# Second layer's probabilities turned by DMA and bounded by ScalarE, fourth layer's mask added by VectorE, maxima turned in one transpose

## The chip, the cores and the metric

The kernel runs on one core of one Trainium2 chip. The time is device microseconds of one execution of the whole program; lower is better. A core has five engines that run their own instruction queues in order: TensorE (matmuls and transposes into PSUM; its weight loads are listed apart as PEld), VectorE (DVE), ScalarE (ACT), GpSimd (POOL) and SyncE (SP), whose queue here issues all DMAs. An engine stops at an instruction whose inputs are not there, and everything behind it in that queue waits too.

## The reference, cut to what matters

Four layers of attention and feed-forward follow one another on `x` of 16 batches x 128 tokens x 256 features, with 16 heads of 16 features. Only the second and the fourth layer, and the softmax of the third, matter here.

The second layer quantizes: scores of rounded queries and keys, a softmax, and the probabilities rounded to whole numbers from 0 to 255 before the product with the rounded values.

```
def _fq(x, delta, zp, n_bits):
    xi = _round_ste(x / delta) + zp
    xq = jnp.clip(xi, 0.0, 2.0 ** n_bits - 1.0)
    return (xq - zp) * delta
...
sim = einsum(_fq(q, dq, 128., 8), _fq(k, dk, 128., 8)) * SCALE
attn = softmax(sim)
out = einsum(_fq(attn, dw, 0.0, 8), _fq(v, dv, 128.0, 8))
```

This attention comes twice in the layer, first of the tokens to themselves, then to the context. The third layer adds a mask times -1e9 to the scores (a 128 x 128 mask in its first attention, one row of keys for each batch in its second). The fourth layer's second attention puts minus infinity where a 128 x 128 boolean mask is set:

```
scores = einsum('bhqd,bhkd->bhqk', q, k) * scale
if mask is not None:
    scores = jnp.where(mask[None, None], -jnp.inf, scores)
attn = softmax(scores)
out = einsum('bhqk,bhkd->bhqd', attn, v)
```

## The kernel before, in words

The 16 batches are worked in 8 groups of two (`GB = 2`), so a tile of tokens is 128 partitions x 2 x 256. `group(g)` lists a group's whole way through the four layers as steps. A step names an engine (or several that could do it), an assumed duration, the blocks it reads and writes, and a function that issues its instructions. All eight groups may be under way at once (`LIVE = 8`).

The order on every engine is fixed when the program is built. `Plan.order` plays the steps through with their assumed durations, always takes the ready step that could begin first (then by its level plus a number from the table `LEADS`, one for each group and stage), and gives it a place in memory. SBUF data lie in one `arena` of 348 units of 512 bytes a partition; each section of a group's work says how many buffers of a kind (`e`, `eT`, `eb`, `mt`, `w`) it may hold. A step on SP ends, for the plan, 2.2 us (`LOAD`) after its assumed duration, plus what the step names as its fourth entry. PSUM has four `pw` slots of 2 KB a partition and one `ps` slot of 8 KB, which holds all 16 heads' scores of one batch.

The second layer (`quantized_attention`, then `attention`) takes each of the two batches of a group in two halves of 8 heads, `c = 0, 1`: 2 attentions x 8 groups x 2 batches x 2 halves are 64 halves and 32 batches. For a half:
- TensorE has made the scores in `ps` (L833, bf16); VectorE takes the maxima (L1099) and subtracts them into `e` (L1112); ScalarE makes exponentials (L1118); VectorE makes the sums and their inverses (L1124 to L1127); POOL multiplies by them and adds `MAGIC` = 12582912.0, which rounds to a whole number (L1133).
- VectorE bounds the result at 255, takes `MAGIC` off again and writes bf16 into `eb` (L1137).
- TensorE turns the 8 heads' squares into a `pw` slot (L905), ScalarE or VectorE copies them out to `eT` (L910, L911).
- When both halves are there, TensorE multiplies with the values in `products` (L879): 16 bf16 matmuls of 128 columns, four at a time side by side on 32 columns of the array each. ScalarE scales the result by `dwv` (L1143).

The third and fourth layers use `plain_attention` (4 attentions, 64 batches in all). For a batch it makes the scores twice: queries on the partitions, to find each query's maximum for each head, then keys on the partitions with the maxima already taken off, so that the exponentials need no turn. In between the 16 maxima of each query are split into three bf16 pieces (`split`, L1261 to L1264), which lie in `mq` as four squares of 128 columns; four transposes (L1271) and one copy (L1275) bring them to `mt`. Four bf16 matmuls of 512 columns with the constant `three` (L844, from `laid`) then lay the negated maxima into all of `ps`, and the f32 scores accumulate onto them (L833). `laid` and the scores work on four strips of 32 partitions at a time.

Masks come in two ways. With `mask` (third layer's first attention) VectorE adds it while it moves the scores from `ps` to `e` or `eT` (L1246, L1295); the maxima are then taken from `e` (L1251) and the exponentials from `eT` (L1299). With `masked` and `masked_T` TensorE lays the mask into `ps` ahead of the scores, as a product with `ident_b` (L844); the maxima (L1236) and the exponentials (L1302) then read `ps`. The fourth layer's second attention does the latter, with the mask `m3` and its turned form `m3T` in bf16; there a row may have all keys masked, and one small instruction (L1239) puts such maxima to zero.

Of the kernel before, what the change touches and what calls it, by code (L numbers as in the profile page):

```python
# [16 lines left out]
P = 128  # L17
# [49 lines left out]
SLOTS = {"sm": (64, 46), "row": (128, 12), "pw": (2048, 4), "ps": (8192, 1), "mq": (1024, 4)}  # L67
# [8 lines left out]
    [83, 27, 167, 130, 306, 193, 74, 226, 213, -45, 163, -53, 159, -84, 116, -64, 214, 400, 286, 283],  # L76
    [-69, -856, -114, -260, -60, 57, -165, -14, -2, -22, -386, -90, 144, -71, -260, -59, -586, -159, -213, -106],
    [49, -47, -11, 314, -162, 407, 51, 168, -361, -27, -172, 141, -4, -107, 36, 5, -54, 235, 78, 92],
    [-16, -228, 250, -173, -19, 106, 36, 203, -176, 14, 164, 2, 299, -144, 10, 309, -45, 154, 150, -1],
    [210, 166, 422, 222, 201, 790, 324, 499, 569, 334, 435, 116, 502, 205, 259, 760, 536, 716, 652, 178],  # L80
    [330, 158, 210, 147, 392, 517, 262, 488, 490, 57, 292, 77, 380, 208, 348, 38, 542, 447, 523, 1141],
    [267, 148, 130, 158, 333, 376, 220, 605, 204, -29, 43, 216, 340, 164, 196, 435, 324, 999, 754, 951],
    [288, 156, 593, 320, 407, 313, 255, 389, 233, 323, -30, 86, 440, 164, 213, 583, 372, 760, 452, 550],
# [344 lines left out]
def decoder_stack_kernel(ctx: ExitStack, tc: tile.TileContext, a: dict, out: bass.AP):  # L428
# [19 lines left out]
    G.memset(magic, MAGIC)  # L448

# [40 lines left out]
    m3 = const.tile([P, S], BF16, tag="m3", name="m3")  # L490
    m1T = const.tile([P, S], F32, tag="m1T", name="m1T")
    m3T = const.tile([P, S], BF16, tag="m3T", name="m3T")
# [3 lines left out]
    three = const.tile([P, P], BF16, tag="three", name="three")  # L496
    mod = const.tile([P, 32], F32, tag="mod", name="mod")
# [28 lines left out]
    def prepare():  # L526
# [5 lines left out]
        def steps_of_quantization():  # L532
# [8 lines left out]
            V.tensor_tensor(dwv, d[:, :, 2], d[:, :, 3], ALU.mult)  # L541

# [6 lines left out]
        def masks():  # L549
# [4 lines left out]
            G.tensor_tensor(three, three, mod[:, 2:3].to_broadcast([P, P]), ALU.add)  # L554

            G.tensor_scalar(m1, m1, -1.0e9, 1.0, ALU.mult, ALU.mult)

        step([("POOL", 2.5, masks)], reads=[raw, dl_token], writes=[mask_token], least=110.0)


        for dst, n, src, eye, dtype in ((m1T, S, m1, ident, F32), (kmT, B, km, ident[:B, :B], F32), (m3T, S, m3, ident_b, BF16)):
# [305 lines left out]
    def products(eTs, vz, j, po, ones=False):  # L867

        def issue():
            for c in range(2):
                for i in range(2):
                    for s in range(4):
                        if ones:
                            lhsT = ones2[:, i, :]
                        else:
                            lhsT = vz.ap()[:, j, 4 * c + s, 2 * i : 2 * i + 2, :].rearrange("p a d -> p (a d)")
                        T.matmul(  # L879
                            po.ap()[32 * s : 32 * s + 32, 2 * ones + c, :], lhsT=lhsT,  # L880
                            rhs=eTs[c].ap()[:, 2 * s + i, :], start=(i == 0), stop=(i == 1),
                        )

        return issue

    def attention(x, wo, begin, soft, out_of, vz, dtype, after):


        plan.enter(after=after, w=1, oT=1, e=2, eT=2, **({"r": 1} if dtype == F32 else {"eb": 1}))
        wo = weight(wo)  # L890
        oT = block("m", [P, 2, NT], role="oT")
        for j in range(GB):
            ps, held = begin(j)
            eTs = []
            for c in range(2):
# [3 lines left out]
                per = 4 if dtype == F32 else 8  # L899
                for q0 in range(0, 8, per):  # L900
                    pt = block("pw", [P, per, S], dtype)

                    def turn(pt=pt, e=e, q0=q0):
                        for q in range(per):
                            T.transpose(pt.ap()[:, q, :], e.ap()[:, q0 + q, :], ident if dtype == F32 else ident_b)  # L905
# [291 lines left out]
    def plain_attention(x, qxT, kvT, ws, biases, mask=None, masked=None, cost=0.9, masked_T=None, key_mask=None, held=(), may_be_empty=False, there=None):  # L1197
# [29 lines left out]
        def batch(j):  # L1227
# [52 lines left out]
            def below(ps, mt=mt):  # L1280
                if masked_T is not None:
                    laid(ps, *masked_T)
# [187 lines left out]
```

## Time and profile before

| | |
|---|---|
| Time, median of 3 runs | 1461.03 us (1458.67 to 1462.03) |
| The profiled execution's own time | 1458.82 us |
| Its span, first to last instruction | 1456.7 us |
| TensorE busy | 1398.3 us, 96% of the span |
| VectorE busy | 1010.9 us, 69% |
| ScalarE busy | 849.7 us, 58% |
| POOL busy | 633.3 us, 43% |
| Mean granted TensorE clock | 0.993 |
| DMA, mean | 75 GB/s |

A profile is one execution taken by the hardware profiler. A line of it names the engine, the line of the program, the operation, the tile that is written and those that are read with their shapes (partitions x elements, or rows x columns of the array for TensorE), and a count; then the busy time, the mean duration in ns of one, and the idle time of the engine just before, with what ended it. Matmuls are pipelined, so a block's duration contains its drain, and the start of the next block comes earlier than its end. An f32 matmul or weight load shows as two instructions.

### The profile page before, as it was taken

How to read it: one execution, taken by the hardware profiler on the slowest of the kernel's cores; microseconds unless marked ns; L12 is line 12 of the kernel's file. 1: busy time of each engine (PE TensorE's matmuls, PEld its weight loads, DVE VectorE, ACT ScalarE, POOL GpSimd, SP SyncE). 2: the span in 40 equal slices, each digit the busy share in tenths (PEclk: the TensorE clock that was granted, in tenths of full speed). 3: DMA queues.
4: the chain of work that ended last, by engine and by line, in shares of the span. 5: the costliest groups of instructions: out<-in, count | busy, mean ns of one | idle time of the engine just before them, and what ended most of it. 6: DMA issues, size and time to landing. Idle time of an engine off the chain costs nothing. (4 is left out here: it accounts for less than half of the span.)

```text
span 1456.7 us, 35756 instructions
## 1 busy us (share of the span) xinstructions
PE 1398.3 (96%) x14771; PEld 1141.3 (78%) x14771; DVE 1010.9 (69%) x1555; ACT 849.7 (58%) x1490; POOL 633.3 (43%) x1415
## 2 busy tenths in 40 slices
PE   8899998999899999899999999999999999999998
PEld 6677887878678888687878777777878888787777
DVE  1665788898988779767764976779478766556431
ACT  4565676766776656565554665657556454445552
POOL 2232857455777446524432542545634234243210
PEclk9999998999999999999999999999999999999999
DMA  6566513412432122112211532211210111100000
GB/s 207 138 171 192 188 48 102 117 34 67 125 90 95 44 67 70 56 52 66 84 38 45 160 101 97 85 55 56 73 45 2 42 38 66 31 31 2 2 9 23
DMA packets 138386, 109.67 MB, mean 75 GB/s; under 512 B 72288, under 2 KB 127472, under 8 KB 138096
## 3 DMA queue, kind: packets, MB, share of 16 engines
q1 hardware_dynamic: 138224, 107.40, 24.5%
q8 instruction: 116, 1.90, 0.5%
q14 instruction: 46, 0.38, 0.1%
HBM read 80.11 MB, written 27.26 MB: 74 GB/s over the span
## 5 line engine op out<-in xcount | busy, mean ns | idle before, releaser
L688 PE MATMUL pw<-arena 128*128 128x256 f32 x2048 | 484.2, 387 | 7.3 <-ACT arena L654 3.1
L675 PE MATMUL pw<-arena 128*128 128x256 f32 x2048 | 480.9, 385 | 7.8 <-ACT arena L663 2.5
L688 PEld LDWEIGHTS pw<-arena 128*128 128x128 f32 x2048 | 383.0, 192 | 68.8 <-issue 9.3
L675 PEld LDWEIGHTS pw<-arena 128*128 128x128 f32 x2048 | 379.2, 191 | 71.0 <-issue 10.0
L1133 POOL TENSOR_SCALAR arena<-arena,sm 128x128 f32<-128x128 f32 x512 | 195.9, 403 | 107.7 <-DVE sm L1127 73.4
L1314 DVE RECIPROCAL arena<-pw 128x256 f32<-128x256 f32 x64 | 112.1, 1752 | 104.0 <-PE pw L879 86.8
L734 POOL TENSOR_TENSOR arena<-arena,rows 128x512 f32<-128x512 f32 x107 | 137.7, 1289 | 89.7 <-ACT arena L721 74.0
L833 PE MATMUL ps<-arena 32*128 32x128 f32 (+2 forms) x3328 | 153.0, 309 | 2.8 <-DVE arena L1112 1.1
L1236 DVE TENSOR_REDUCE sm<-ps 128x16 f32<-128x2048 f32 x48 | 109.6, 2283 | 36.3 <-PE ps L833 33.8
L833 PEld LDWEIGHTS ps<-arena 32*128 32x128 f32 x3072 | 116.1, 186 | 20.4 <-issue 12.0
L696 DVE TENSOR_TENSOR arena<-pw,arena 128x512 f32<-128x512 f32 x88 | 60.3, 685 | 101.2 <-PE pw L688 99.7
L801 ACT ACTIVATE arena<-pw,cols_sb 128x256 f32<-128x256 f32 x184 | 78.0, 472 | 68.3 <-PE pw L675 65.5
L1261 POOL CAST mq<-sm 128x16 bf16<-128x16 f32 x58 | 15.8, 273 | 234.2 <-DVE sm L1236 114.6
L710 POOL TENSOR_SCALAR sm<-sm 128x2 f32<-128x2 f32 x88 | 20.6, 234 | 215.0 <-DVE sm L705 200.1
L721 ACT ACTIVATE arena<-arena,sm,sm 128x256 f32<-128x256 f32 x149 | 83.2, 597 | 49.3 <-POOL sm L714 48.7
L663 ACT ACTIVATE arena<-pw,cols_sb 128x256 f32<-128x256 f32 x140 | 72.7, 563 | 50.5 <-PE pw L647 47.0
L1275 ACT COPY arena<-pw 128x512 bf16<-128x512 bf16 x64 | 37.3, 582 | 84.5 <-PE pw L1271 77.6
L879 PE MATMUL pw<-arena 128*32 128x128 f32 (+1 forms) x2560 | 82.9, 265 | 3.4 <-ACT arena L910 3.0
L1099 DVE TENSOR_REDUCE sm<-ps 128x8 f32<-128x1024 f32 x64 | 77.6, 1213 | 9.8 <-PE ps L833 9.5
L1302 ACT ACTIVATE arena<-ps 128x1024 f32<-128x1024 f32 x64 | 64.1, 1025 | 33.1 <-PE ps L833 30.3
L647 PE MATMUL pw<-ident,arena 128*128 128x128 f32 x416 | 66.8, 286 | 15.1 <-DMA arena<-in_x_dram 5.1
L910 ACT COPY arena<-pw 128x1024 bf16<-128x1024 bf16 x56 | 56.3, 1011 | 41.9 <-PE pw L905 37.2
(142 smaller groups left out, 1993.8 us busy)
## 6 DMA issues: line engine op xcount, KB each, us to landing
arena<-in_L_xattn_ff_w_dram SPq DMA_DIRECT2D x38, 256.0 KB, 3.0
mha<-arena SPq DMA_DIRECT2D x16, 512.0 KB, 4.5
ca<-arena SPq DMA_DIRECT2D x16, 512.0 KB, 3.9
arena<-mha SPq DMA_DIRECT2D x16, 512.0 KB, 4.4
arena<-ca SPq DMA_DIRECT2D x16, 512.0 KB, 4.5
dqkv<-arena SPq DMA_DIRECT2D x8, 768.0 KB, 4.0
arena<-dqkv SPq DMA_DIRECT2D x16, 384.0 KB, 4.3
arena<-in_L_xattn_W_dram SPq DMA_DIRECT2D x24, 256.0 KB, 2.8
```

The lines of the kernel that those rows point to most:

```text
L663: ("ACT", 0.54, lambda c=c: A.activation(dst.ap()[:, c, :], ps.ap()[:, c, :], AF.Identity, bias=biases(c), scale=scales(c))),
L675: T.matmul(ps.ap()[:, m, :], lhsT=w.ap()[:, k, m * P : (m + 1) * P], rhs=t.ap()[:, k, :], start=(k == 0), stop=(k == 1),)
L688: T.matmul(ps.ap()[:, j, :], lhsT=lhs(k, j) if lhs else t.ap()[:, k, j * S : (j + 1) * S], rhs=w.ap()[:, k, :], start=start and j + k == 0 ...
L721: ("ACT", 0.6, lambda j=j: A.activation(xh.ap()[:, j, :], x.ap()[:, j, :], AF.Identity, bias=nb.ap()[:, j : j + 1], scale=rstd.ap()[:, j : ...
L734: ("POOL", 1.33, lambda: G.tensor_tensor(dst.ap(), src.ap(), row(name), op)),
L801: "ACT", 0.47, lambda ps=ps, h=h, m=m, bias=bias: A.activation(h.ap()[:, m, :], ps.ap()[:, m, :], func, bias=bias),
L833: T.matmul(ps.ap()[:, s, c] if i is None else ps.ap()[:, s, c, i], lhsT=left(r, c) if i is None else left(r, c, i), rhs=right(r, c), start ...
L879: T.matmul(po.ap()[32 * s : 32 * s + 32, 2 * ones + c, :], lhsT=lhsT, rhs=eTs[c].ap()[:, 2 * s + i, :], start=(i == 0), stop=(i == 1),)
L1099: step([("DVE", 1.22, lambda: V.tensor_reduce(paired(m.ap()), ps.ap()[:, :, c], AX.X, ALU.max, negate=True))], reads=[ps], writes=[m])
L1133: G.tensor_scalar(e.ap()[:, q, :], e.ap()[:, q, :], r.ap()[:, q : q + 1], MAGIC, ALU.mult, ALU.add)
L1236: V.tensor_reduce(m.ap(), ps.ap().rearrange("p s c i k -> p (s c i) k"), AX.X, ALU.max, negate=True)
L1314: step([("DVE", 1.75, lambda po=po, r=r: V.reciprocal(r.ap(), po.ap()[:, 2:4, :]))], reads=[po], writes=[r])
```

## The change

- **Second layer.** POOL's result is no longer bounded by VectorE. ScalarE computes relu(`MAGIC` + 255 - e), which is 255 minus the rounded probability, zero where that would be negative: what is missing to 255. It goes to `eb` in bf16, of which there are now two buffers. A transposing DMA from SP's queue turns all 8 squares from `eb` straight into `eT`; the transposes on TensorE and the copies out of PSUM are gone. `products` adds, for every value tile, a second matmul with a constant tile of -255 (`n255`), and `dwv` is negated, so that the sum is that of the probabilities again.
- **Fourth layer, second attention.** The mask goes the way of the third layer's: `mask=(m3, m3T)` in f32, added by VectorE. The instruction for rows with all keys masked becomes a step of its own.
- **Maxima.** The three pieces of the 16 maxima go into one square of 128 columns, 12 columns in each of the four strips; one transpose and one copy of 128 columns move them. Four constants `three_of` pick the pieces of one of four heads each. In place of four matmuls of 512 columns there are sixteen of 128, issued between the scores of the head that they belong to; each region of `ps` is now started and ended by its own pair.
- **The rest.** `mq` slots shrink from 1024 to 256 bytes, some constants are made once, two assumed durations are changed, and the whole table `LEADS` has other numbers.

```diff
-SLOTS = {"sm": (64, 46), "row": (128, 12), "pw": (2048, 4), "ps": (8192, 1), "mq": (1024, 4)}
+SLOTS = {"sm": (64, 46), "row": (128, 12), "pw": (2048, 4), "ps": (8192, 1), "mq": (256, 4)}
...
 LEADS = [
-    [83, 27, 167, 130, 306, 193, 74, 226, 213, -45, 163, -53, 159, -84, 116, -64, 214, 400, 286, 283],
...
+    [79, -243, 396, 61, 306, 431, -218, 552, 246, -1043, 475, -1, 382, -725, -212, 120, 529, 352, 259, 257],
...
+    top = const.tile([P, 1], F32, tag="top", name="top")
+    G.memset(top, MAGIC + 255.0)
+    n255 = const.tile([P, S], BF16, tag="n255", name="n255")
+    G.memset(n255, -255.0)
...
+            V.tensor_scalar(dwv, dwv, -1.0, None, ALU.mult)
...
+            for f in range(4):
+                t = three_of[:, f, :]
+                G.tensor_tensor(t, mod[:, 3 * f : 3 * f + 1].to_broadcast([P, P]), mod[:, 3 * f + 1 : 3 * f + 2].to_broadcast([P, P]), ALU.add)
+                G.tensor_tensor(t, t, mod[:, 3 * f + 2 : 3 * f + 3].to_broadcast([P, P]), ALU.add)
...
                 for i in range(2):
-                    for s in range(4):
...
+                    for n in range(1 if ones or not missing else 2):
+                        for s in range(4):
...
+                                rhs=n255 if n else eTs[c].ap()[:, 2 * s + i, :], start=i == n == 0, stop=i == 1 and n == missing,
...
-        plan.enter(after=after, w=1, oT=1, e=2, eT=2, **({"r": 1} if dtype == F32 else {"eb": 1}))
+        plan.enter(after=after, w=1, oT=1, e=2, eT=2, **({"r": 1} if dtype == F32 else {"eb": 2}))
...
-                            T.transpose(pt.ap()[:, q, :], e.ap()[:, q0 + q, :], ident if dtype == F32 else ident_b)
...
-                            ("ACT", 0.6 if dtype == F32 else 1.2, lambda pt=pt, eT=eT, q0=q0: A.copy(eT.ap()[:, q0 : q0 + per, :], pt.ap())),
...
+                step(
+                    [("SP", 1.2, lambda e=e, eT=eT: nc.sync.dma_start_transpose(out=eT.ap(), in_=e.ap().rearrange("p q k -> p (q k)")), None, 1.0)],
+                    reads=[e], writes=[eT],
+                )
...
-            step([("DVE", 0.76, lambda: V.tensor_scalar(eb.ap(), e.ap(), MAGIC + 255.0, -MAGIC, ALU.min, ALU.add))], reads=[e], writes=[eb])
+            step([("ACT", 1.05, lambda: A.activation(eb.ap(), e.ap(), AF.Relu, bias=top, scale=-1.0))], reads=[e], writes=[eb])
...
-            m, rest, mq = small(16), small(16), block("mq", [P, 4, P], BF16)
+            m, rest, mq = small(16), small(16), block("mq", [P, P], BF16)
...
-            def turn(pt=pt, mq=mq):
                 for f in range(4):
-                    T.transpose(pt.ap()[:, f, :], mq.ap()[:, f, :], ident_b)
...
+            step([("PE", 0.1, lambda pt=pt, mq=mq: T.transpose(pt.ap(), mq.ap(), ident_b))], reads=[mq], writes=[pt], holds=[mt])
...
+                    c, i = divmod(f, 2)
+                    for part in (0, 1) if i else (1, 0):
+                        for s in range(4):
+                            r = strip(s)
+                            T.matmul(
+                                pT.ap()[:, s, c, i], lhsT=kz.ap()[r, c, i, tok] if part else three_of[r, f, :],
+                                rhs=qT.ap()[r, c, tok] if part else mt.ap()[r],
+                                start=masked_T is None and part == 1 - i, stop=(f == 3 or masked_T is None) and part == i,
+                            )
...
-        plain_attention(x, hT, hT, weights(SQUARE[3][4:]), bias_qk[ATT[3]], masked=lambda j: lambda ps: laid(ps, lambda s: ident_b, lambda s: fourfold(m3)), cost=1.85,
-            masked_T=(lambda s: ident_b, lambda s: fourfold(m3T)), may_be_empty=True)
+        plain_attention(x, hT, hT, weights(SQUARE[3][4:]), bias_qk[ATT[3]], mask=(m3, m3T), may_be_empty=True)
```

## The prediction

> **What bounds the kernel now.** I read the page's table of busy time first, then the chain that ended last, the windows of 100 us, TensorE's groups with shapes kept apart, its timeline, and the waits. From the page, in that order: the engines' busy time, the chain's shares by engine and by line, and the queue that carries the DMAs:
>
> ```profile
> PE 1398.3 (96%) x14771; PEld 1141.3 (78%) x14771; DVE 1010.9 (69%) x1555; ACT 849.7 (58%) x1490; POOL 633.3 (43%) x1415
> ...
> PE 29%; DVE 1%; ACT 0%; issue 0%; ACTq 0%
> ...
> q1 hardware_dynamic: 138224, 107.40, 24.5%
> ```
>
> TensorE is busy 96% of the span; the piece of chain that could be followed back (31% of the span, its last part) is TensorE's for 29 of 31 points. So time leaves this kernel by way of TensorE's instruction stream, or of the 58.4 us in which it idles. The windows (length, then busy us of PE, PEld, DVE, ACT, POOL, the granted clock, the DMA share) show where that idle time is and where the second engine comes close:
>
> ```profile
> 0.00:100.00 100.00, 84.99 (x685) 70.64 (x686) 43.09 (x108) 56.89 (x133) 27.56 (x55) 0.98 0.63 173
> 200.00:300.00 100.00, 93.69 (x729) 76.50 (x729) 85.99 (x144) 72.75 (x138) 61.56 (x137) 0.95 0.34 91
> 500.00:600.00 100.00, 97.57 (x1160) 78.11 (x1164) 84.81 (x116) 59.57 (x110) 61.35 (x142) 0.98 0.21 65
> 700.00:800.00 100.00, 97.70 (x1228) 80.97 (x1227) 62.23 (x92) 52.69 (x84) 37.37 (x83) 1.00 0.16 53
> ```
>
> 15 us of the idle time lie in the first 100 us, some 2.4 in each 100 us from 400 on. VectorE reaches 85 to 90 between 200 and 600, no more than 80 after it.
>
> TensorE's busy column overlaps between groups (the groups add up to more than 1398), so I price by the timeline: the start of a block to the start of the next one, over all blocks that no wait follows. Two stretches show it:
>
> ```profile
> 508.29 0.62 PE L905 MATMUL pw<-ident_b,arena 128*128 128x128 bf16 x8
> 508.74 0.39 PE L1271 MATMUL pw<-ident_b,mq 128*128 128x128 bf16 x4
> 509.06 0.41 PE L879 MATMUL pw<-arena 128*32 128x128 bf16 x16
> 509.39 3.72 PE L675 MATMUL pw<-arena 128*128 128x256 f32 x16
> ...
> 603.25 1.02 PE L844 MATMUL ps<-m3T,ident_b 128*128 128x512 bf16 x4
> 604.21 0.40 PE L844 MATMUL ps<-arena,three 32*128 32x512 bf16 x4
> 604.43 1.06 PE L833 MATMUL ps<-arena 32*128 32x128 f32 x32
> 605.42 0.23 PEld L1271 LDWEIGHTS <-mq 128*128 128x128 bf16 x4
> ```
>
> The medians: eight turns of L905 0.46 us, four of L1271 0.23, sixteen bf16 products of L879 0.34, a four-matmul mask by `ident_b` 0.96, the four with `three` 0.225, the f32 scores behind them 0.99, and eight bf16 scores of 256 columns (L833) 0.33.
>
> **The change part by part.** The sum is made against the profiled execution's own 1458.82 us, a span of 1456.7 and 2.1 around it; the median of the three runs, 1461.03, lies 0.15% above it.
>
> *Turns leave TensorE.* 64 blocks x 0.46 = -29.4 us. VectorE's bound and cast goes (L1137, 64 x 0.784 = 50.1 us), so do the copies that emptied the turns (ScalarE 56 x 1.01 = 56.3, VectorE 8 x 0.68 = 5.4). ScalarE gains 64 Relus from SBUF to SBUF; the nearest row is L1299, 1.056 us for the same size: +67.6. ScalarE is idle 42% of the span, which hides that; uncovered, it would cost the same 67.6. [...]
>
> *The products* of both signs: 16 more bf16 matmuls in each of 32 blocks, 32 x 0.34 = +10.9.
>
> *The DMA.* 64 transfers of 256 KB on SP's queue, each behind a Relu; behind each stand the next weight loads. An issue takes about 0.37 us in the rows of L634, so 24 us of a queue that mostly waits. TensorE waits for no weight load at all now (its DMA waits are for `x` and `ctx` alone), so a load has room; one that comes late costs up to its 2.7 to 4.9 us of landing. No transposing DMA is in the trace. From below 2.0 us, the fastest landing of the small `do` stores; from above 7.8, the slowest of the 512 KB ones. I take 4.4, the median of the `ca` and `mha` loads at twice the bytes, since a turn is likelier to move at half a copy's pace than at a copy's. The plan books 1.2 + 2.2 + 1.0 = 4.4 from issue to landing, so at that value nothing stalls. What shows slack now: 26 of 32 product blocks found the turned copies ready, and the median distance from the latest such copy's end to the products' start is 1.8 us, a floor for the slack:
>
> ```profile
> PE pw L879 <- ACT arena L910: 3.0, 4, 0.9
> ```
>
> The path of one batch gets longer, 0.78 + 0.61 + 1.01 = 2.4 before, 1.06 + 4.4 = 5.4 after; seven other groups cover that.
>
> *The fourth layer's masks* leave TensorE: 32 blocks x 0.96 = -30.7. VectorE takes 32 additions and 32 half reductions before the split and 32 additions after it (39.0 each by L1246, L1251 and L1295), and loses 16 reductions of 2.283: +117.0 - 36.5 = +80.5. Half of its exponentials (L1302, 1.025) read SBUF instead (1.056): +1.0. The one `ps` slot is held 3 x 1.22 instead of 2.29 by the reduction (`e` has a single buffer) and 2.44 instead of 2.05 by the exponentials, +1.8 us a batch, against 2 x 0.96 of mask matmuls no longer in it: even. VectorE in all: -55.5 + 80.5 = +25.0, 1036 us, 73% of the new span. The relief falls between 100 and 1110 us, the load on the later stretch, where VectorE has room.
>
> *Maxima in one turn.* 64 x 0.75 x 0.23 = -11.0. ScalarE's copies shrink from 0.58 (37.3 in all) to some 0.30 (below the 0.38 of L1172's 256 columns): -18, so ScalarE ends near 849.7 - 56.3 + 67.6 + 1.0 - 18 = 844. In place of the four matmuls with `three` (0.225) stand sixteen bf16 ones of 128 columns among the f32 scores, eight by eight. Bounds: 16 x 0.021 = 0.34 by the column-tiled products, 16 x 0.041 = 0.66 by the row-tiled bf16 scores with twice the columns. Half the columns on the second row's tiling lies between: I take 0.45, +0.225 x 64 = +14.4 (ends +7.4 and +27.8).
>
> *Once:* eight more POOL instructions among the masks, 8 x 0.40 = 3.2 us, in a stretch in which POOL is busy 27.6 of 100; the masks are first read at 308 us. Two memsets ahead: nothing.
>
> *The order.* Every row of `LEADS` is new, so the planner interleaves otherwise. What that does to TensorE's 58.4 us of idle time no row can say; I leave it as it is.
>
> Sum on TensorE: -29.4 - 30.7 - 11.0 + 10.9 + 14.4 = -45.8. 1458.8 - 45.8 = **1413 us**.
>
> **The rivals.**
> *The turns land late (slower).* Products stand in TensorE's own order, so a late landing stops everything behind them, once in each of 32 blocks. The plan's 4.4 and the slack of 1.8 are free; the gain of 45.8 is gone at 45.8 / 32 = 1.4 us more, a landing of 7.6. At 8.8, twice the loads of 512 KB, it is 32 x 2.6 = 83 us: 1496. For it: the slowest 512 KB landing, 7.8, and a DMA share of 63% in the first 100 us. Against: 256 KB land in 2.7 to 4.9, and the share is 9 to 41% where most turns will be. [...]
> *VectorE takes back half.* In stretches like 200 to 600, where it stands at 85 to 90, the additions of the fourth layer may delay other groups' reductions. Half of 45.8 lost: 1436. Against: the relief of 55.5 lies there, the load elsewhere.
> *The new order also saves idle time.* Outside the first 100 us there are 43.4 us of it; half gone gives 1391. Waits of 5.2 us before L905 and 2.4 before L1271 go with their blocks.
> *TensorE's work was not the bound,* so that nothing happens: 1459. The chain speaks against it.
>
> **How the numbers follow.** Likeliest, 0.55: TensorE's sum as above, 1403 to 1428 by the bounds of the maxima (-7, +13) and a few us of idle time either way. New order better, 0.13: 1385 to 1403. Half lost, 0.14: 1428 to 1456. No change, 0.02. Late turns, 0.16: above 1462. So faster 0.82, same 0.02, slower 0.16; the limit is 0.2%, 2.9 us, about what the measurement can tell. The range from 1386 to 1462 leaves out the late turns and little below.
>
> **What would show it.** L905's group and the masks by `ident_b` gone; L879's bf16 blocks at 32 matmuls and 0.68 us; TensorE's busy time near 1352 with idle time near 58; VectorE near 1036; the turns landing within 6.2 us of issue, and a wait of the bf16 products for a DMA near nothing. I am wrong if that wait is long (late turns), if TensorE's idle time before L1236's and L1246's successors grows (VectorE), or if the scores with maxima take more than 1.65 us a batch.

## The result, and the profile after

The changed kernel takes 1441.1 us (median of four runs, 1440.3 to 1445.8) against 1461.5 for the kernel before in the same session: a ratio of 0.988, 95% interval 0.9862 to 0.9897. So it is faster, by 15 to 20 us going by the interval and by 20.4 going by the medians, where 48 were forecast. The profiled execution took 1440.7 us, with a span of 1438.9.

The page of the changed kernel, engines' busy time and the chain's shares by engine:

```profile
PE 1358.0 (94%) x15219; PEld 1116.4 (78%) x15219; DVE 1042.8 (72%) x1608; ACT 837.6 (58%) x1480; POOL 596.8 (41%) x1393
...
PE 79%; DVE 9%; ACT 2%; issue 1%; POOL 1%; DMA 1%; SPq 0%; DVEq 0%; ACTq 0%; POOLq 0%
```

TensorE's busy time fell by 40.3 us (1398.3 to 1358.0), and the span by 17.8. The difference is idle time: 80.9 us now, 58.4 before. The windows of the changed kernel (length, then busy us of PE, PEld, DVE, ACT, POOL, granted clock, DMA share, GB/s) show where it lies:

```profile
200.00:300.00 100.00, 85.51 (x720) 69.42 (x720) 83.06 (x148) 80.19 (x145) 71.20 (x164) 0.90 0.50 130
300.00:400.00 100.00, 86.89 (x702) 71.61 (x701) 83.76 (x141) 64.12 (x96) 67.68 (x158) 0.93 0.36 84
400.00:500.00 100.00, 92.61 (x928) 77.03 (x927) 76.16 (x123) 69.52 (x124) 56.20 (x131) 0.97 0.30 72
...
700.00:800.00 100.00, 90.08 (x1094) 73.09 (x1094) 85.68 (x121) 60.92 (x96) 39.04 (x93) 0.97 0.25 65
800.00:900.00 100.00, 99.79 (x1233) 81.86 (x1232) 72.45 (x110) 58.23 (x96) 45.26 (x105) 1.00 0.26 70
...
334.00:340.00 6.00, 0.00 (x0) 0.00 (x0) 5.79 (x14) 1.65 (x2) 5.53 (x15) 0.50 0.00 0
340.00:343.00 3.00, 1.38 (x4) 0.68 (x4) 2.97 (x4) 1.89 (x4) 2.83 (x9) 0.50 0.54 78
343.00:346.00 3.00, 2.65 (x6) 2.18 (x7) 2.93 (x5) 2.83 (x4) 0.70 (x3) 0.50 0.31 59
```

Between 200 and 500 TensorE idles 35.0 us, before 14.6; from 600 to 800 it idles 18.4, before 4.7. After 800 it idles 7.0 us, 4.0 of them at the end, before 16.8. The last three lines are a close view of one gap and what follows it.

The clock column falls too. Laid on the stretches that show a granted clock of 0.50 throughout, the windows give these sums (length, then the busy us), first for the kernel before, in four stretches, then for the changed one, in eight:

```profile
sum 20.48, PE 18.21 PEld 13.48 DVE 18.56 ACT 9.75 POOL 10.55; mean PE 4.55 PEld 3.37 DVE 4.64 ACT 2.44 POOL 2.64
sum 58.03, PE 38.02 PEld 27.55 DVE 51.95 ACT 37.10 POOL 44.53; mean PE 4.75 PEld 3.44 DVE 6.49 ACT 4.64 POOL 5.57
```

They are 53.88 to 57.29, 224.54 to 234.78, 371.32 to 374.73 and 593.18 to 596.60 before, and 53.43 to 56.84, 200.20 to 213.85, 292.36 to 299.19, 333.32 to 346.97, 408.41 to 415.24, 609.80 to 613.21, 684.89 to 688.31 and 783.88 to 790.71 after. So 38.0 us of TensorE's work ran at the half clock, before 18.2. In the close view, six f32 matmuls take 2.65 us there, 0.44 each; the sixteen at 509.39 in the kernel before, at a granted clock of 1.00, take 3.72, 0.23 each. If all such work takes about twice its time, the half clock costs 19.0 us of TensorE's busy time now and 9.1 before: an estimate of 9.9 more.

The largest waits of TensorE (total, times, longest):

```profile
PE pw L658 <- ACT arena L732: 19.3, 10, 7.1
PE ps L844 <- DVE arena L1113: 11.4, 4, 4.5
PE pw L686 <- ACT arena L674: 8.2, 9, 1.8
PE pw L892 <- DMA arena<-arena: 5.3, 2, 5.0
```

L732 is the scaling of a layer norm on ScalarE, L658 the transposes behind it. (L732 and L658 of this kernel are L721 and L647 of the kernel before, where the same pair cost 3.4 us; L844 and L892 were L833 and L879.) The wait for a turned tile is there only twice. The longest idle stretch of the changed kernel, and a fourth-layer batch, in its timeline (start, length, engine and line, what it does, then the idle time ahead and its releaser):

```profile
332.66 0.40 PE L844 MATMUL ps<-arena 32*128 32x256 bf16 x8 [2.01 <-DVE arena L1113]
337.88 1.15 ACT L1139 ACTIVATE arena<-arena,top 128x1024 bf16<-128x1024 f32 x1 [4.09 <-POOL arena L1134]
339.50 1.09 ACT L732 ACTIVATE arena<-arena,sm,sm 128x256 f32<-128x256 f32 x2 [0.47 <-POOL sm L725]
340.15 1.39 PE L658 MATMUL pw<-ident,arena 128*128 128x128 f32 x4 [7.09 <-ACT arena L732]
343.35 5.49 PE L686 MATMUL pw<-arena 128*128 128x256 f32 x16 [1.81 <-ACT arena L674]
...
1386.86 0.50 PE L1292 MATMUL ps<-arena 32*128 32x128 f32 x8
1387.18 0.29 PE L1292 MATMUL ps<-arena,three_of 32*128 32x128 bf16 x8
1387.29 0.68 PE L1292 MATMUL ps<-arena 32*128 32x128 f32 x16
1387.79 0.29 PE L1292 MATMUL ps<-arena,three_of 32*128 32x128 bf16 x8
1387.91 0.46 PE L1292 MATMUL ps<-arena 32*128 32x128 f32 x8
1388.29 0.23 PE L1274 MATMUL pw<-ident_b,mq 128*128 128x128 bf16 x1
```

From 333 to 340 us nothing is ready for TensorE. ScalarE stands for 4.09 us in front of the new Relu (L1139), which waits for GpSimd's scaling of the same tile (L1134); the layer norm's scaling is behind it on ScalarE's queue. The Relu is not the last to hold it here: the line of L732 also has 0.47 us of waiting for L725, the last of GpSimd's small steps for the same layer norm, which stand behind L1134 on GpSimd's queue. The last six lines are one batch's scores with the maxima mixed in: 1.43 us from the first to the turn behind them. The transposes and matmuls right behind the gap are slow; that is taken up at the end.

The group of the Relu (busy us, mean ns of one, then ScalarE's idle time ahead of it and its main releaser):

```profile
L1139 ACT ACTIVATE arena<-arena,top 128x1024 bf16<-128x1024 f32 x64 | 73.4, 1147 | 41.4 <-POOL arena L1134 35.5
```

The turns by DMA (issue on SP's queue in ns as minimum, median and maximum, then the landing in us):

```profile
L913 SPq DMA_TRANSPOSE arena<-arena x64: 1231/1238/2224, 191.3 to 1000.5; - x64
...
DMA to landing us min/median/max: 3.0/3.1/6.6
```

### The profile page after: what moved, and what is told of

It reads as the page before. It is cut to its first block, busy times and chain, and to the rows that moved or that the text cites. A ratio compares the mean times of both kernels' runs of the same rounds, so it can differ in the third digit from the quotient of the medians.

```text
span 1438.9 us, 36661 instructions
## 1 busy us (share of the span) xinstructions
PE 1358.0 (94%) x15219; PEld 1116.4 (78%) x15219; DVE 1042.8 (72%) x1608; ACT 837.6 (58%) x1480; POOL 596.8 (41%) x1393
## 4 chain that ended last, share of the span: by engine, by line
PE 79%; DVE 9%; ACT 2%; issue 1%; POOL 1%; DMA 1%; SPq 0%; DVEq 0%; ACTq 0%; POOLq 0%
PE pw L699 27%; PE pw L686 27%; PE pw L892 9%; PE ps L1292 6%; PE ps L844 5%; PE pw L658 3%; DVE arena L1113 2%; DVE sm L1100 2%; DVE sm L1125 1%; DVE arena L962 1%; DVE sm L1243 1%; PE pw L987 1%; DVE arena L1250 1%; DVE sm L1255 1%; DVE sm L715 0%
## 5 line engine op out<-in xcount | busy, mean ns | idle before, releaser
L1134 POOL TENSOR_SCALAR arena<-arena,sm 128x128 f32<-128x128 f32 x512 | 186.7, 386 | 106.1 <-DVE sm L1128 71.9
L812 ACT ACTIVATE arena<-pw,cols_sb 128x256 f32<-128x256 f32 x188 | 80.0, 471 | 77.7 <-PE pw L686 70.9
L732 ACT ACTIVATE arena<-arena,sm,sm 128x256 f32<-128x256 f32 x151 | 83.8, 595 | 31.8 <-POOL sm L725 30.7
L1292 PE MATMUL ps<-arena 32*128 32x128 f32 x2048 | 97.4, 299 | 3.3 <-DVE sm L1243 2.5
L1139 ACT ACTIVATE arena<-arena,top 128x1024 bf16<-128x1024 f32 x64 | 73.4, 1147 | 41.4 <-POOL arena L1134 35.5
L892 PE MATMUL pw<-arena 128*32 128x128 f32 (+1 forms) x2560 | 88.5, 266 | 9.1 <-DMA arena<-arena 5.3
L844 PE MATMUL ps<-arena 32*128 32x256 f32 (+1 forms) x1280 | 84.7, 371 | 12.0 <-DVE arena L1113 11.4
L658 PE MATMUL pw<-ident,arena 128*128 128x128 f32 x416 | 69.0, 292 | 27.1 <-ACT arena L732 19.3
L1292 PEld LDWEIGHTS ps<-arena 32*128 32x128 f32 x2048 | 75.8, 188 | 23.0 <-issue 10.4
L721 POOL TENSOR_SCALAR sm<-sm 128x2 f32<-128x2 f32 x88 | 17.2, 195 | 183.7 <-DVE sm L716 179.5
L1310 ACT ACTIVATE arena<-arena 128x1024 f32<-128x1024 f32 x64 | 66.5, 1054 | 41.5 <-DVE arena L1306 40.5
L872 POOL MEMSET arena<- 128x512 f32 (+1 forms) x48 | 25.0, 526 | 155.4 <-PE pw L699 56.9
L1119 ACT ACTIVATE arena<-arena,sc 128x1024 f32<-128x1024 f32 x62 | 70.6, 1147 | 31.3 <-DVE arena L1113 31.2
L1250 DVE TENSOR_TENSOR arena<-ps,m 128x1024 f32<-128x1024 f32 x64 | 78.0, 1219 | 12.4 <-PE ps L844 8.0
```

The costliest lines, as they stand in the source:

```text
L658: T.transpose(p[:, c, j * S : (j + 1) * S], s[:, j, c * P : (c + 1) * P], ident)
L732: ("ACT", 0.6, lambda j=j: A.activation(xh.ap()[:, j, :], x.ap()[:, j, :], AF.Identity, bias=nb.ap()[:, j : j + 1], scale=rstd.ap()[:, j : ...
L812: "ACT", 0.47, lambda ps=ps, h=h, m=m, bias=bias: A.activation(h.ap()[:, m, :], ps.ap()[:, m, :], func, bias=bias),
L844: T.matmul(ps.ap()[:, s, c] if i is None else ps.ap()[:, s, c, i], lhsT=left(r, c) if i is None else left(r, c, i), rhs=right(r, c), start ...
L892: T.matmul(po.ap()[32 * s : 32 * s + 32, 2 * ones + c, :], lhsT=lhsT, rhs=n255 if n else eTs[c].ap()[:, 2 * s + i, :], start=i == n == 0, ...
L1134: G.tensor_scalar(e.ap()[:, q, :], e.ap()[:, q, :], r.ap()[:, q : q + 1], MAGIC, ALU.mult, ALU.add)
```

## The experiments

Kernels named b_ are the kernel before with an edit, in the order of before: its `LEADS` and the prices of its steps are kept, so that every engine gets its steps in the old sequence. (The change moves more than two of these prices: the masks' from 2.5 to 5.0, the products' from 0.24 to 0.46, that of the scores with maxima from 1.1 to 1.15, and those of the maxima's turn and copies; the new steps have prices of their own.) Kernels named a_ are the changed kernel with an edit, in the changed kernel's order. Each was timed in turns with the kernel before, so each has its own ratio.

**The parts in the old order.** My first theory was that the new order had cost the missing gain. Each part alone, and all three, were put into the kernel before; to make room for the new tiles, pools of small buffers were cut (`sm` from 46 to 22 among them), the mask part adds into one fixed tile `e3`, and the turn part has a single `eb`. The edits are the matching lines of the change, here their core:

```diff
 # b_max
-T.transpose(pt.ap()[:, f, :], mq.ap()[:, f, :], ident_b)      # four of them
+T.transpose(pt.ap()[:, 0, :], mq.ap(), ident_b)
 # b_mask
-masked=lambda j: lambda ps: laid(ps, lambda s: ident_b, lambda s: fourfold(m3))
+V.tensor_tensor(paired(e3), ps.ap()[:, :, c], m3..., ALU.add)
 # b_turn
-T.transpose(pt.ap()[:, q, :], e.ap()[:, q0 + q, :], ident_b)
+nc.sync.dma_start_transpose(out=eT.ap(), in_=e.ap().rearrange("p q k -> p (q k)"))
 # b_all: the three together
```

> Before's order on every engine (its LEADS, its assumed durations), with the maxima part alone: one turn of 128 columns, a copy of 128 columns, sixteen bf16 matmuls of three_of among the f32 scores. The sum of the prediction gives -11.0 + 14.4 = +3.4 us, so 1464 to 1466 by the theory that the order took the missing gain. If the mixed scores cost more than 0.45 us over the f32 ones, the rival that the price of the maxima was too low, it is 1470 and above; by the column-tiled row it is 1457.

> Before's order, with the fourth layer's mask alone moved to VectorE (additions through one fixed buffer in place of e). Theory that the order took the gain: TensorE's -30.7 us comes through, 1431 to 1437. Rival that VectorE takes it back (80 us more of its work, at the old places in its queue): 1445 to 1462.

> Before's order, with the second layer's part alone: Relu on ScalarE at the place of VectorE's bound, the transposing DMA in SP's queue at the place of the turn, products of both signs. TensorE loses 29.4 and gains 10.9: 1443 if the slack of 1.8 us and the rest of the queue cover the later landing (some 4.3 us after issue against 1.7 for turn and copy). Rival of late turns: 32 x (2.6 - 1.8) = 26 us come back, 1465 to 1470, with TensorE waiting for the DMA ahead of the products.

> Before's order with all three parts. Theory that the new order took the missing gain: 1413 to 1425, TensorE's idle time near 58 us. Rival that the parts themselves take it back whatever the order: 1438 or more, like the changed kernel, with idle time near 81 us.

| kernel | us | ratio, 95% interval | TensorE busy |
|---|---|---|---|
| b_max | 1462.2 | 1.0009, 0.9997 to 1.002 | 1405.5 |
| b_mask | 1494.5 | 1.0238, 1.0219 to 1.0258 | 1390.6 |
| b_turn | 1514.6 | 1.0378, 1.0353 to 1.0403 | 1400.3 |
| b_all | 1541.5 | 1.0578, 1.0543 to 1.0612 | 1390.0 |

The waits of TensorE in b_mask:

```profile
PE pw L1279 <- POOL mq L1272: 9.5, 7, 1.9
PE ps L834 <- DVE e L1238: 6.8, 7, 2.1
PE ps L845 <- DVE e L1238: 3.9, 3, 1.7
```

In b_turn the line of the turns by DMA, and who waited for it (total, times):

```profile
L910 SPq DMA_TRANSPOSE arena<-arena x64: 1231/1232/2731, 149.3 to 1155.5; - x64
...
  PE pw L885: 26.5, 13
  ACT arena L1142: 25.9, 8
```

The theory fell, and from the unexpected side. In the old order the change isn't a smaller gain but a loss of 81 us: the turns land after their products are due (26.5 us), and the next Relu (L1142 in b_turn) waits for the landing because its buffer is still being read (25.9); VectorE's additions hold up the scores in the one `ps` slot (6.8 and 3.9 in b_mask), and the split behind them the turn of the maxima (9.5). Only the maxima come out near nothing. In the order that the changed kernel brings along, made with the new steps' prices and with two `eb`, the same steps are 100 us faster (1541.5 against 1441.1). Part of that may be the buffer and not the order; the two were not tried apart. Nor is it idle time alone: b_all and the changed kernel issue the same 15219 matmul instructions, but TensorE is busy 1390.0 us in b_all and 1358.0 in the changed kernel, at a mean granted clock of 0.961 against 0.980. The same goes for b_mask: 30.7 us of matmuls are gone, TensorE's busy time falls by only 7.7, and the mean clock is 0.976 against 0.993 before.

**What a microsecond of TensorE is worth.** If replaced work and order can do so much, the other half of the sum is to be tested too: is a microsecond taken from TensorE a microsecond of time? Here TensorE's work is simply left out. In b_skipmask the fourth layer isn't masked; in b_skipturn one turn of eight is made and copied over the square; in a_skipprod the 255 isn't taken off; in a_late half of the row-sum matmuls of the fourth layer's second attention are missing, and the others sum neighbouring heads too.

```diff
 # b_skipmask
-masked=lambda j: lambda ps: laid(ps, ...m3), masked_T=(...m3T), may_be_empty=True
+cost_T=2.1, may_be_empty=True
 # b_skipturn
-for q in range(per):
+for q in range(1):
 # a_skipprod
-products(eTs, vz, j, po, missing=True)
+products(eTs, vz, j, po)
 # a_late
-for i in range(2):
+for i in range(1 if few else 2):        # few: row sums of the fourth layer's second attention
```

> Before's order, with the fourth layer's 32 mask blocks on TensorE left out and nothing in their place, so that layer is not masked. It asks what a microsecond taken from TensorE is worth by itself. Theory of the prediction (TensorE's stream is the bound, one for one): -30.7 us, 1428 to 1433, and then VectorE's additions cost the whole distance to the 1494 of the mask part. Rival that another engine or a wait stands right behind TensorE: half of it or less, 1445 or more.

> Before's order, with seven of each eight turns of the second layer left out; the copy spreads the first square over all eight, so the attention's probabilities are wrong. TensorE loses 64 x 7/8 x 0.46 = 25.7 us and nothing else changes. One for one: 1433 to 1437. Rival that another engine or a wait stands right behind TensorE: 1447 or more.

> The changed kernel in its own order; the 16 matmuls with n255 are left out of each of the 32 product blocks of the second layer (the 255 is not taken off), so TensorE loses 32 x 0.34 = 10.9 us. One for one it is 1430. At the rates of the two leave-out runs in the old order (0.35 and 0.70) it is 1433 to 1437. If other engines end the waits there, 1441.

> The changed kernel in its own order; half of the row-sum matmuls of the fourth layer (8 of 16 f32 matmuls in each of 32 blocks, the last of four heads summed together with its neighbour left out) are not issued, about 8 x 0.055 = 0.44 us a block by the plan's price, 14 us in all, nearly all of them after 740 us. There TensorE idles hardly at all from 800 us on, so by the theory of places the rate is near one: 1427 to 1431. If the rate is the same 0.4 as for the products with n255, 1435 to 1436.

| kernel | TensorE work left out | us | ratio, 95% interval | gained | rate |
|---|---|---|---|---|---|
| b_skipmask | 30.7 (32 x 0.96) | 1441.1 (before 1462.7) | 0.9863, 0.9842 to 0.9885 | 21.6 | 0.70 |
| b_skipturn | 25.7 (7/8 of 29.4) | 1453.8 (before 1462.7) | 0.9942, 0.9927 to 0.9956 | 8.9 | 0.35 |
| a_skipprod | 7.0 | 1437.1 (changed 1441.1) | 0.985, 0.9835 to 0.9865 | 4.4 | 0.6 |
| a_late | 7.0 | 1436.3 (changed 1441.1) | 0.9835, 0.9814 to 0.9856 | 6.6 | 0.9 |

Two expectations counted the work wrongly. A product block takes 0.56 us in the changed kernel and 0.34 without the matmuls of `n255`, so a_skipprod leaves out 32 x 0.22 = 7.0 us, not 10.9. The edit of a_late reaches one of the fourth layer's two attentions, 16 batches, so it leaves out 16 x 0.44 = 7.0 (a block of row sums takes 0.99 us in the changed kernel and 0.55 here), not 14. The gain of these two is the difference between their ratio and the changed kernel's 0.988, times 1460 us, since they were timed in other sessions than it; it is uncertain by 3.4 and 4.0 us to each side, so their rates can be told apart neither from each other nor from one. In the old order it is clear that b_skipturn's 0.35 is far below one, and below b_skipmask's 0.70, which is below one too. The windows of b_skipturn show where the rest went:

```profile
200.00:300.00 100.00, 90.03 (x664) 72.34 (x663) 86.08 (x146) 73.29 (x140) 62.01 (x137) 0.95 0.34 91
300.00:400.00 100.00, 92.39 (x996) 74.56 (x999) 89.23 (x144) 65.76 (x127) 59.74 (x136) 0.95 0.27 78
400.00:500.00 100.00, 95.69 (x581) 78.20 (x571) 85.76 (x139) 65.70 (x104) 66.34 (x139) 0.98 0.29 86
```

Where the turns stood, TensorE is now busy 278.1 of 300 us instead of 285.4, while VectorE's column has hardly moved: the time taken from TensorE turned into waiting, in place. Some of it also came back as slower matmuls: over the run TensorE's busy time fell by 17.5 us (1398.3 to 1380.8) where 25.7 were left out, and the mean granted clock went from 0.993 to 0.987. So one for one was wrong in the old order; in the new one the two runs leave it open.

**Who stands behind TensorE in the changed kernel?** Four candidates, each taken away in the changed kernel's order: late turns, VectorE, GpSimd, and the layer norms' chain. a_nowait reads `n255` in both halves of the product, so that no product waits for a turn. a_nomask leaves out the fourth layer's additions, with its exponentials moved to the additions' place; a_thinmask makes them for one head of eight and leaves every step where it is. a_recip copies where the plain attentions take reciprocals, b_recip does so in the kernel before. a_thinq makes the second layer's maxima and subtractions on an eighth of the scores, a_thinpool scales a tile with one head's factor in one instruction, a_thinboth does both. a_nonorm lets the layer norms' scaling read constants, while statistics and roots are still issued. a_every joins a_nowait, a_thinmask, a_thinboth, a_nonorm and short multiplications for the reciprocals.

```diff
 # a_nowait
-rhs=n255 if n else eTs[c].ap()[:, 2 * s + i, :]
+rhs=n255 if missing else eTs[c].ap()[:, 2 * s + i, :]
 # a_thinmask (a_nomask: not at all)
-V.tensor_tensor(paired(eT.ap()), pT.ap()[:, :, c], mask[1]..., ALU.add)
+V.tensor_tensor(eT.ap()[:, 7], pT.ap()[:, 3, c, 1], mask[1], ALU.add)
 # a_recip, b_recip
-V.reciprocal(r.ap(), po.ap()[:, 2:4, :])
+V.tensor_copy(r.ap(), po.ap()[:, 2:4, :])
 # a_thinq
-V.tensor_reduce(paired(m.ap()), ps.ap()[:, :, c], AX.X, ALU.max, negate=True)
+V.tensor_reduce(paired(m.ap()), ps.ap()[:, :, c, :, 0:16], AX.X, ALU.max, negate=True)
-V.tensor_tensor(paired(e.ap()), ps.ap()[:, :, c], wide(m.ap()), ALU.add)
+V.tensor_tensor(e.ap()[:, 7], ps.ap()[:, 3, c, 1], m.ap()[:, 7:8].to_broadcast([P, S]), ALU.add)
 # a_thinpool
-for q in range(8): G.tensor_scalar(e.ap()[:, q, :], e.ap()[:, q, :], r.ap()[:, q : q + 1], MAGIC, ...)
+G.tensor_scalar(e.ap(), e.ap(), r.ap()[:, 0:1], MAGIC, ALU.mult, ALU.add)
 # a_nonorm
-bias=nb.ap()[:, j : j + 1], scale=rstd.ap()[:, j : j + 1]
+bias=plain[:, 0:1], scale=plain[:, 1:2]
```

> The changed kernel in its own order, with the second layer's products reading the constant tile twice in place of the turned tiles, so the output of that attention is wrong; the DMAs still run, but no matmul waits for them. Theory of late turns as the taker: 1420 or less. Rival that the turns are in time once the order knows of them: 1433 to 1438, the 5.3 us that TensorE was seen to wait for them.

> The changed kernel in its own order, with the fourth layer's mask additions left out (the reductions and exponentials read PSUM, and a tiny copy stands where the reduction was), so that layer is not masked. VectorE loses some 73 us. Theory that VectorE's additions hold the missing 26 us: 1413 to 1422. Rival that the order as planned holds it, whichever engine: 1430 to 1441.

> The changed kernel in its own order; the fourth layer's additions of the mask are made for one head of eight only (both sides, 128 of 1024 columns; reductions and exponentials read that head eight times, every step keeps its place), so VectorE loses 64 additions of 1.22 us and gets 64 of some 0.2: about -64 us. If VectorE's additions hold the missing gain (the rival 'VectorE takes back half'), the time falls by 20 to 28 us, to 1413 to 1421. If they lie beside TensorE's work and the gain is lost elsewhere, it stays within 8 us: 1433 to 1441.

> The changed kernel in its own order; the reciprocals of the plain attentions (64 of 1.75 us on VectorE) are replaced by copies of the same 256 columns (some 0.35 us), so the attention isn't normalised and VectorE loses about 90 us in all layers from 60 us on. If VectorE stands right behind TensorE, TensorE's idle time of 81 us shrinks by 20 to 35 us: 1406 to 1421. If the idle time is made of chains of steps and not of VectorE's load, no more than 8 us: 1433 to 1441.

> The same edit in the kernel before: copies in place of the 64 reciprocals. By the theory that TensorE bounds one for one, nothing beyond the idle time of 58 us can be had and VectorE's load is hidden: 1455 to 1461. If VectorE was already right behind TensorE in the kernel before, in the stretches where it is 85 to 90% busy, 10 to 20 us: 1441 to 1451.

> The changed kernel in its own order; in the second layer VectorE's maximum reads one eighth of the scores and its subtraction makes one head of eight, which the exponential reads eight times: 126 steps of 1.22 us become some 0.25, about -120 us of VectorE between 180 and 990 us, most of it between 200 and 600, and every chain of a batch gets 2 us shorter. If VectorE's steps hold the idle time of 35 us between 200 and 500, a good part goes: 1410 to 1425. If other steps do, 1433 to 1441.

> The changed kernel in its own order; GpSimd scales the eight heads of a tile of the second layer with one instruction and one head's scale in place of eight of 0.37 us: about -100 us of GpSimd, and each batch's chain 1.5 us shorter. If GpSimd's load (71% between 200 and 300) holds the idle time, by way of the layer norms that stand behind it on its queue: 1415 to 1428. If not, 1435 to 1441.

> Both edits at once. If each engine only hides the other, the two together bring far more than their sum: 1400 to 1415. If the idle time is the order's, made of waits for single chains (layer norm, diagonal, landing) that these edits don't touch, it stays above 1430.

> The changed kernel in its own order; all statistics of the layer norms and GpSimd's four small steps behind them are still issued in their places, but the scaling reads two constants in place of their results (x is scaled by 0.25, not normalised), so it waits for x alone. TensorE's idle time ahead of the transposes, put down to the scaling, is 42 us on 28 occasions in the trace. If the statistics and GpSimd's queue are what makes the scaling late, 1410 to 1425. If the scaling is late by its place on ScalarE's queue, or the next wait stands right behind, 1433 to 1441.

> The changed kernel in its own order with all the single edits at once: VectorE's additions of the fourth layer and its maxima and subtractions of the second thinned to an eighth, the 64 reciprocals replaced by short multiplications, GpSimd's scaling by one instruction a tile, the products of the second layer not waiting for the turned copies, and the layer norms' scaling reading constants (attention and norms are not normalised). TensorE's instructions are the same, VectorE loses some 260 us of 1043 and GpSimd some 115 of 597. If the waits hide one another, most of the 45 us of idle time that the changed kernel has beyond the first 100 us and the end goes: 1390 to 1412. If the idle time is TensorE's own order against ScalarE and the loads, no more than thinning VectorE and GpSimd in the second layer alone gave: 1422 to 1432.

| kernel | VectorE, GpSimd busy | us | ratio, 95% interval |
|---|---|---|---|
| the changed kernel | 1042.8, 596.8 | 1441.1 | 0.988, 0.9862 to 0.9897 |
| a_nowait | 1043.1, 595.6 | 1442.9 | 0.9867, 0.9851 to 0.9884 |
| a_nomask | 974.1, 600.3 | 1451.8 | 0.9929, 0.9914 to 0.9943 |
| a_thinmask | 985.6, 600.5 | 1442.2 | 0.9888, 0.987 to 0.9906 |
| a_recip | 963.2, 599.7 | 1441.1 | 0.9878, 0.9864 to 0.9893 |
| b_recip | 929.7, 635.7 | 1456.3 | 0.9982, 0.9969 to 0.9995 |
| a_thinq | 933.3, 596.0 | 1436.2 | 0.9835, 0.9817 to 0.9852 |
| a_thinpool | 1044.6, 481.8 | 1441.5 | 0.9867, 0.9848 to 0.9886 |
| a_thinboth | 927.3, 482.8 | 1430.1 | 0.9793, 0.9776 to 0.981 |
| a_nonorm | 1042.7, 598.2 | 1441.8 | 0.9885, 0.9858 to 0.9912 |
| a_every | 785.6, 483.4 | 1432.8 | 0.9804, 0.9787 to 0.982 |

Late turns are not it: without the wait nothing changes. VectorE's additions are not it: 57 us less on VectorE, the same time. The reciprocals lie mostly where TensorE is already full (46 of 64 after 800 us); in the kernel before, 81 us less on VectorE gave 2.6. GpSimd alone gives nothing clear of the noise, VectorE in the second layer 5 to 7 us, and the two together 11 to 13, by the medians and by the ratios. That may be more than their sum, each hiding a little of the other, but the intervals don't settle it, and it is far from all. a_nomask is 10 us slower with less work; its exponentials stand earlier on ScalarE's queue, and I read no more from it than that moving a step can cost more than its work was worth. And with all of it at once VectorE is 257 us shorter and GpSimd 113, and the time is still 1432.8. The page of a_every, engines' busy time:

```profile
PE 1361.3 (95%) x15219; PEld 1118.5 (78%) x15219; DVE 785.6 (55%) x1608; ACT 832.5 (58%) x1480; POOL 483.4 (34%) x947
```

So none of the work that was taken from VectorE and GpSimd holds the greater part of TensorE's idle time; TensorE idles 68.6 us even here (1429.9 - 1361.3). What is left is how the steps are chained in their written order, or ScalarE, whose work no run made much shorter. TensorE's longest wait of a_every points there:

```profile
PE pw L661 <- ACT arena L735: 19.8, 9, 4.6
```

That is the layer norms' scaling again, and it waits for nothing much itself (6.0 us in all): it is late by its place on ScalarE's queue, behind Relus, exponentials and other steps. ScalarE is busy 80.2 of the 100 us from 200 on in the changed kernel, 72.8 in the kernel before. Its load and its order were not told apart.

a_nonorm shows one such place, the same as the long gap above. Its timeline (L1142, L735 and L661 there are L1139, L732 and L658):

```profile
336.85 1.15 ACT L1142 ACTIVATE arena<-arena,top 128x1024 bf16<-128x1024 f32 x1 [4.09 <-POOL arena L1137]
337.91 1.08 ACT L735 ACTIVATE arena<-arena,plain 128x256 f32<-128x256 f32 x2
...
338.54 1.39 PE L661 MATMUL pw<-ident,arena 128*128 128x128 f32 x4 [6.52 <-ACT arena L735]
```

The scaling now needs no statistics, and yet it starts only when the Relu ahead of it on ScalarE's queue is done, which waited 4.09 us for GpSimd; TensorE waits 6.52 us for it. (The 42 us of the expectation add the waits of the weight loads, 23.0, to those of the matmuls, 19.3, which lie over each other; TensorE can win 19.3 at most there.) Over the run the Relu made ScalarE wait 35.5 us for GpSimd (23 times); the bound and cast that it replaces made VectorE wait 7.3 (8 times).

Whether the Relu's place costs much in all stays open: that it heads the queue is shown at this gap, but the kernel with the Relu back on VectorE was not run.

The planner's own account agrees in size with what was measured. Its prices and both tables of `LEADS`, run through the kernels' `order`, give plans of 1442.0 us before and 1419.3 after, 22.7 less, with 1354.7 and 1291.6 us of priced TensorE work in them: 63 us less work, 40 more idle. Those are prices and not measurements, and the forecast, which kept to the profile, didn't use them; but the plan is where the added idle time was written down.

## Why the prediction was right and wrong

**The direction and the bound** held: TensorE is still the busiest with 94%, thinning VectorE and GpSimd gave 13 us at most, faster was given 0.82, and 1441.1 lies in the range of 1386 to 1462. The likeliest time, 1413, was 28 us too low.

**The step that failed** is the one from the sum to the time: "Sum on TensorE: ... 1458.8 - 45.8 = 1413", with "The order ... I leave it as it is" for the idle time. Idle time didn't stay at 58.4, it went to 80.9, 22.5 us more; and behind the gaps more work ran at the half clock, some 9.9 us of busy time, for which the sum has no term. Against these stand 3.7 us that the blocks lost beyond the forecast: 28.7 in all, about what is missing. The leave-out runs show that such a loss needs no new order: in the old one, work taken from TensorE gave back 0.35 and 0.70 of its time. As an account: masks 30.7 x 0.70 = 21.5, turns 29.4 x 0.35 = 10.3, products 7.0 x 0.6 = 4 the other way, maxima 1.3 the other way (b_max): 26 us, against 20 measured. It is an account and no proof, since the rates are from two orders. Why the idle time grew by just this much, and whether this order or any order would have it, stays open.

**The terms.** The turns left TensorE as said. The products' second half was mis-sized: 0.22 a block, +7.0 instead of +10.9. The scores with maxima: 1.43 against 1.215 a block, +13.8, forecast +14.4. One turn of the maxima takes 0.07 instead of 0.23. So by blocks TensorE lost 49.5 us (forecast 45.8) and by its busy time 40.3. The 9.2 between are about the 9.9 that the half clock is estimated to cost. VectorE ended at 1042.8 (forecast 1036), ScalarE at 837.6 (844): right, though a Relu took 1.147 us and not 1.056.

**The turns' landing** was taken as 4.4 us and came out at 3.1 (3.0 to 6.6), and the rival of late turns didn't happen in the new order. It happened in the old one (b_turn). The slack of 1.8 us that I read from the kernel before was thus no cover; the new order's distances are. The half of a copy's pace behind the 4.4 was my estimate, and no run shows it. The issue was forecast at 0.37 us of the queue and takes 1.24; TensorE's waits put down to a weight load are one of 0.2 us.

**"ScalarE is idle 42% of the span, which hides that"** was true of the sum and not of the place: what stood behind the waiting Relu on ScalarE's queue, the layer norms' scaling, was not named.

**"VectorE takes back half"** gave 1436, close to the time, for a reason that fell: the additions cost nothing that can be measured in the new order. The closeness is luck.

**The signs of being wrong** were none of them seen: the products waited only 5.3 us for a DMA, the scores with maxima took 1.43 us, and TensorE's waits for the maxima and their split came to 6.1 us, 5.5 before. They were signs of the rivals; for the idle time itself the prediction only says that it would be near 58, and that is what failed.

## What to carry to other kernels

When the work is issued in an order written down beforehand, time taken off the bounding engine is a ceiling: leave that work out in one run and see what comes back before adding up replacements, since in the old order here it was 0.35 and 0.70 of it. Where the kernel carries its own planner, its plan is worth reading first: it gave 22.7 us where the blocks gave 45.8. New gaps on TensorE cost more here than their own length: work behind them ran at a granted clock of 0.50, which took about 2.5 us more behind the one of 7.09 us and, by the estimate above, 9.9 in all. A share of idle time on another engine covers a moved step only where it stands; look at what it will wait for and at what is queued behind it. And a change whose steps take other engines or other latencies should be judged with an order made for it: the same steps were 81 us slower in the old one and, with a second `eb`, 20 faster in the new.

## What the runs showed of the hardware

TensorE's granted clock falls within a gap, that of 7.09 us from 333.06 to 340.15 in the close windows above: it is 1.00 up to 333.32, and 0.50 from there on and for some 7 us behind the gap, to 346.97. There four transposes took 1.39 us (0.60 at 355.19, at a clock of 1.00), and sixteen f32 matmuls, which ran partly at the half clock, 5.49 (3.72 at 509.39 in the kernel before). This gap of 7 us thus cost about 2.5 more. All twelve stretches at 0.50 are close to 3.41 us long or to two, three or four times that (3.41 to 3.42, 6.83, 10.24 and 13.65). Each of the eight in the changed kernel starts inside a wait of TensorE of 0.96 to 7.09 us, or at most 1.25 us behind the end of one.

A DMA that turns 256 KB of bf16 within SBUF, 128 x 1024, held SP's queue for 1.24 us at its issue and landed after 3.1 us, about as the plain loads of 256 KB (2.7 to 4.1, by the medians of their groups of two loads or more).
